# Mixture of experts on one core: Strassen's form for all first layers from the start, and the gates spread over the partitions by transfers

## The chip, the cores and the metric

The kernel runs on one core of a Trainium2 chip. The metric is the device time of one execution in microseconds (us); lower is better. The kernel before takes 3385.79 us, the median of three runs (3379.62 to 3386.1). A core has a matrix engine (TensorE, PE in the profile; PEld is its weight load), VectorE (DVE), ScalarE (ACT) and GpSimd (POOL), and SyncE (SP), which here only issues transfers. Each engine works through its own instructions in order; between engines, semaphores hold an instruction back until its operands are there.

## What is computed

Two layers, in fp32, over eight images of 256 channels and 32 x 32 positions. Layer 0 is group norm and a pooled convolution and attention hybrid; the change leaves it alone. Layer 1 takes the positions as 1024 tokens of 256 numbers: layer norm, attention with one head, residual; then layer norm and a mixture of eight experts, residual. The experts are where the change is (x has the shape 8 images x 1024 tokens x 256; batch norms are folded into a scale and a bias per channel in the kernel):

```python
feat = jnp.mean(x, axis=0)
w = jax.nn.softmax(feat @ Wr + br, axis=-1)
h = jnp.einsum('bfd,edh->bfeh', x, W1) + b1
h = jax.nn.relu(_bn(h, g1, be1, m1, v1))
h = jnp.einsum('bfeh,ehk->bfek', h, W2) + b2
h = jax.nn.relu(_bn(h, g2, be2, m2, v2))
y = jnp.einsum('bfeh,ehd->bfed', h, Wo) + bo
return jnp.einsum('bfed,fe->bfd', y, w)
```

The gates `w` (1024 tokens x 8 experts) come from the mean over all eight images. So they are known only when the last image's attention and layer norm are done, while first and second layers of the experts can run before.

## The kernel before, in words

**The work of the experts.** Activations lie with channels on the 128 partitions, in two halves `k`. The function `experts` (line 1988) cuts the eight images into 16 tiles `hn` of half an image ([128, 2, 512]), and each tile meets eight experts: 128 units, unit `i` being expert `i % 8` of tile `i // 8`. A unit has three layers:

- `first(i)` (2126) is the plain first layer: two `half`s (2107), each of two fp32 matmul calls of 128 x 128 by 512 columns into one PSUM bank "bank" (four buffers, each call is a pair of matmul records in the trace), and a relu on ScalarE that empties it into `h1`.
- `second(i, staged)` (2133) has the same form with `w2` into `h2`. With `staged`, `h2` is stored to its place `h2d[i]` in DRAM; `fetch(i)` (2144) brings it back.
- `weigh(i)` (2236) multiplies `h2` by the gates of its expert, a tile `gb` of [128, 8 experts, 1024 tokens] with each gate repeated on all partitions, and makes the combinations `t3`; `third(i)` (2242) adds the product with `wo` into the PSUM banks "y", over all eight experts of a tile. After the eighth the residual is added on VectorE and the tile is stored to `out`.

**Strassen's form.** `first7(i)` (2222) and `third` use seven products of quarter size for a 256 x 256 matrix by 512 columns, in place of eight (Winograd's form of Strassen's scheme): `products` (2188) issues seven matmul calls of 256 columns into four banks, `weights` (2171) makes four sums of a weight's blocks on GpSimd once per expert (`s1e`, `s3e`), `combined` (2180) makes four combinations of the operand on VectorE (`t1` once per tile, `t3` once per unit), and `sums` (2209) puts the products together: a copy `p1c` on ScalarE and four sums on VectorE that read the banks (`c`, `u`). In `first7` ScalarE's relu then reads `c`. So a plain first layer's banks are freed by ScalarE, and those of a Strassen first layer by VectorE.

**The order of the work.** The order on each engine is fixed when the program is built, by a planner, the class `Flow` (655). It models every engine's time with `cost` (710) and puts instructions on each engine in the order in which they are called. Threads are generators that yield what they need next; `step(pace)` runs those that are runnable, up to a credit of modelled TensorE time (8.0 per step, `PACE2`), and `finish` drives them until a condition holds. When `experts` starts, layer 1's attention and norms of the last images still run as threads. `experts` adds the thread `gates` (2036): it sums the eight images on VectorE (`featsum`, the other images come through one buffer `feat`), multiplies by the router's weights, forms the softmax and transposes it to `gt`, [8 experts, 1024 tokens]. Then, for each of 16 pairs of half and expert, a matmul with the selecting matrix `sel` spreads one row of `gt` over 128 partitions, and ScalarE copies it from PSUM to `gb`. Last, four products with `bo` give `added`.

While the gates are not complete, the loop at line 2153 runs first and second layers of units 0, 1, 2 and so on, with a planner's step after each; all are plain, and their `h2` go to DRAM. It comes to 22 first and 21 second layers. Then `early.close()` gives back the memory of attention (l1) and of the gates' working tiles (wg), the pool `wp3` and the banks "y" take its place, `s3e` and `s1e` are made, units 0 and 1 are fetched, and the last loop (2277) begins: a third layer, a second layer and a Strassen first layer per turn, and a further third layer while units are still staged in DRAM. 106 first layers have Strassen's form.

The transfers of SP leave in program order: SP waits at each for what it needs, so one that waits holds those behind it.

Of the kernel before, what the change touches and what calls it, by code (L numbers as in the profile page):

```python
# [13 lines left out]
PSUM = bass.MemoryType.PSUM  # L14
# [1970 lines left out]
        advance(after(nb - 1), 10**6)  # L1985


def experts(tc, kit, nb, t2, hn, h2d, w1c, w2_d, wo_d, bnvec, bo_d, gate_d, wrc, consts8, out, f, outer, ended, early):

# [10 lines left out]
    with ExitStack() as ctx:  # L2000
# [22 lines left out]
        f.sp.dma_start(wr, wrc.rearrange("p k e -> p (k e)"))  # L2023
        br = T(wg, [P, NE], "br")
        f.sp.dma_start(br, gate_d[:, 2 * NE :])
        sel = T(wg, [NE, NE * P], "sel")
        f.sp.dma_start(sel, consts8[:, : NE * P])
        bo = T(wg, [NE, C], "bo")
        f.sp.dma_start(bo, bo_d)
        for e in range(NE):  # L2030
            f.sp.dma_start(wo[e], wo_d[:, e])
        gt = T(wg, [NE, HW], "gt")
        gb = T(wp, [P, NE, HW], "gates")
        gated = []

        def gates():

            featsum = T(wp, [P, 2, HW], "featsum")  # L2040
            for b in range(nb):
                yield None, lambda: ended[0] > b, None
                if b == 0:
                    f.sp.dma_start(featsum, hn[0])
                else:
                    h = T(wg, [P, 2, HW], "feat")
                    f.sp.dma_start(h, hn[b])
                    for k in range(2):
# [13 lines left out]
            gate = T(wg, [P, 8, NE], "gate")  # L2062
            yield "DVE", (ps,), None
            f.ve.tensor_scalar(gate, ps, 1.0 / nb, None, ALU.mult)
            f.ve.tensor_tensor(gate, gate, br[:, None, :].to_broadcast([P, 8, NE]), ALU.add)
            red = T(wg, [P, 8], "red")
            f.ve.tensor_reduce(red, gate, AX.X, ALU.max)
            f.ve.tensor_tensor(gate, gate, red.unsqueeze(2).to_broadcast([P, 8, NE]), ALU.subtract)
            yield "ACT", (gate,), None
            f.act.activation(gate, gate, AF.Exp)  # L2070
            yield "DVE", (gate,), None
            f.ve.tensor_reduce(red, gate, AX.X, ALU.add)
            f.ve.reciprocal(red, red)
            f.ve.tensor_tensor(gate, gate, red.unsqueeze(2).to_broadcast([P, 8, NE]), ALU.mult)
            for half in range(2):
                yield "PE", (gate,), "sm"
                ps = T(shared, [P, 512], "sm", bufs=2)
                for ft in range(4):
                    f.pe.transpose(ps[:NE, ft * P : (ft + 1) * P], gate[:, 4 * half + ft, :], kit.ident)
                yield "DVE", (ps,), None  # L2080
                f.ve.tensor_copy(gt[:, half * 512 : half * 512 + 512], ps[:NE, :])
            for half in range(2):
                sl = slice(half * 512, half * 512 + 512)
                for e in range(NE):
                    yield "PE", (gt,), "sm"
                    ps = T(shared, [P, 512], "sm", bufs=2)
                    f.pe.matmul(ps, lhsT=sel[:, e * P : (e + 1) * P], rhs=gt[:, sl], start=True, stop=True)
                    f.act.activation(gb[:, e, sl], ps, AF.Copy)
            added = T(wp, [P, 2, HW], "featsum")
            for m in range(2):  # L2090
                for half in range(2):
                    sl = slice(half * 512, half * 512 + 512)
                    yield "PE", (gt,), "sm"
                    ps = T(shared, [P, 512], "sm", bufs=2)
                    f.pe.matmul(ps, lhsT=bo[:, m * P : (m + 1) * P], rhs=gt[:, sl], start=True, stop=True)
                    f.act.activation(added[:, m, sl], ps, AF.Copy)
            gated.append(added)
# [32 lines left out]
                half(h, w1[e], e, xs[tile_i], 0, 1, m)  # L2130
            loaded(i)

        def second(i, staged):
            _, e, _, _ = where(i)
            h, src = T(work, [P, 2, 512], "h2", bufs=5), h1s.pop(i)
            for m in range(2):
                half(h, w2[e], e, src, 2, 3, m)
                yield
            if staged:
                f.sp.dma_start(h2d[i], h)  # L2140
            else:
                h2s[i] = h

        def fetch(i):
            if i not in h2s:
                h = h2s[i] = T(work, [P, 2, 512], "h2", bufs=5)
                f.sp.dma_start(h, h2d[i])

        total = 2 * nb * NE
        f.spawn(gates(), 7)  # L2150
        n1 = n2 = n3 = 0

        while not gated and n2 < NSTAGED:
            first(n1)
            n1 += 1
            f.step((PACE2, PACE2))
            if n1 > 1:
                for _ in second(n2, True):
                    pass
                n2 += 1  # L2160
                f.step((PACE2, PACE2))
        f.finish(lambda: gated)
        early.close()
        wp3 = ctx.enter_context(tc.tile_pool(name="w3", bufs=1, side="right"))
        psum_y = ctx.enter_context(tc.tile_pool(name="psum_y", bufs=1, space=PSUM, side="right"))

        def blocks(w):

            return w[:, 0, :P], w[:, 1, :P], w[:, 1, P:]

        def weights(w, tag):
            s = T(wp3, [P, 4, P], tag)
            a11, a12, a22 = blocks(w)
            f.pool.tensor_tensor(s[:, 0, :], w[:, 0, P:], a22, ALU.add)
            f.pool.tensor_tensor(s[:, 1, :], s[:, 0, :], a11, ALU.subtract)
            f.pool.tensor_tensor(s[:, 2, :], a11, w[:, 0, P:], ALU.subtract)
            f.pool.tensor_tensor(s[:, 3, :], a12, s[:, 1, :], ALU.subtract)
            return s

        def combined(h, tag):  # L2180

            t = T(wp3, [P, 4, C], tag, bufs=2)
            f.ve.tensor_tensor(t[:, 0:2, :], h[:, :, C:], h[:, 0, :].rearrange("p (n q) -> p n q", n=2), ALU.subtract)
            f.ve.tensor_tensor(t[:, 2, :], h[:, 1, C:], t[:, 0, :], ALU.subtract)
            f.ve.tensor_tensor(t[:, 3, :], h[:, 1, :C], t[:, 2, :], ALU.subtract)
            return t
# [21 lines left out]

        def sums(banks):

            c = T(wp3, [P, 4, C], "c", bufs=2)
            u = T(wp3, [P, 2, C], "u", bufs=2)
            p26, p57, p34 = (banks[i].rearrange("p (u q) -> p u q", u=2) for i in (0, 2, 3))
            p1 = T(wp3, [P, 1, C], "p1c", bufs=2)
            f.act.activation(p1[:, 0, :], banks[1][:, :C], AF.Copy)
            f.ve.tensor_tensor(c[:, 0::2, :], p1.to_broadcast([P, 2, C]), p26, ALU.add)
            f.ve.tensor_tensor(u, c[:, 2:3, :].to_broadcast([P, 2, C]), p57, ALU.add)
            f.ve.tensor_tensor(c[:, 3, :], u[:, 1, :], p57[:, 0, :], ALU.add)
            f.ve.tensor_tensor(c[:, 1:3, :], u, p34, ALU.add)
            return c.rearrange("p (m n) q -> p m (n q)", m=2)  # L2220

        def first7(i):
# [10 lines left out]
            if e == NE - 2 and tile_i + 1 in xs:  # L2233
                ts[tile_i + 1] = combined(xs[tile_i + 1], "t1")

        def weigh(i):
            _, e, _, sl = where(i)
            h = h2s[i]
            f.ve.tensor_tensor(h, h, gb[:, e : e + 1, sl].to_broadcast([P, 2, 512]), ALU.mult)
            h2s[i] = h, combined(h, "t3")  # L2240

        def third(i):
            tile_i, e, b, sl = where(i)
# [10 lines left out]
                f.sp.dma_start(out[b].rearrange("(k p) n -> p k n", p=P)[:, :, sl], t)  # L2254
                ys.pop(tile_i)

        s1, s3 = {}, {}
        for i in range(NE):
            s3[i] = weights(wo[i], f"s3e{i}")
            e = (n1 + i) % NE  # L2260
            s1[e] = weights(w1[e], f"s1e{e}")

        def thirds(count):
            nonlocal n3
# [7 lines left out]
                    n3 += 1  # L2272

        for i in range(2):
            fetch(i)
        weigh(0)
        while n3 < total:
# [18 lines left out]
def tile_conv_attn_hybrid(  # L2296
# [34 lines left out]
    t1, t2, hn = ([T(dram, [P, 2, HW], f"{name}_{b}") for b in range(nb)] for name in ("t1", "t2", "hn"))  # L2331
    w1c = T(dram, [P, NE, 2, C], "w1c")
    wrc = T(dram, [P, 2, NE], "wrc")
    h2d = [T(dram, [P, 2, 512], f"h2_{i}") for i in range(2 * nb * NE)]

    assert 8 * nb <= NBOUND
    bnvec = T(cpool, [P, 4 * 2 * NE], "bnvec")
    bounds = [T(cpool, [P, NBOUND], f"bound{i}") for i in range(2)]
    flag = T(cpool, [P, 1], "flag")
    last = partial(experts, tc, kit, nb, t2, hn, h2d, w1c, w2_d, wo_d, bnvec, bo_d, gate_d, wrc, consts8, out)  # L2340
    with ExitStack() as early:
        l1 = early.enter_context(tc.tile_pool(name="l1", bufs=1, side="right"))
        shared = early.enter_context(tc.tile_pool(name="psum_l1", bufs=1, space=PSUM, side="right"))
# [130 lines left out]
```

## Time and profile before

The profiled execution has a span of 3379.9 us and a mean TensorE clock of 0.980 of full speed. Instructions are named by the tiles they write and read, since all of them are recorded by one helper line (L668): "bank<-hn,w1e" is a plain first layer or a Strassen one's product of the operand itself, "bank<-t,s1e" a product of two sums, "y<-..." the third layers, "sm" the banks of attention and of the gates.

| Engine | busy us | share of the span | instructions |
|---|---|---|---|
| TensorE | 3195.0 | 95% | 15270 |
| VectorE | 2267.8 | 67% | 3890 |
| ScalarE | 1695.4 | 50% | 2222 |
| GpSimd | 520.7 | 15% | 644 |

| Group (out<-in) | count | mean ns |
|---|---|---|
| TensorE bank<-h,w2e, 512 columns | 1024 | 594 |
| TensorE bank<-hn,w1e, 256 and 512 columns | 600 | 447 |
| TensorE bank<-t,s1e, 256 columns | 636 | 379 |
| ScalarE h<-bank, relu of 512 columns | 300 | 772 |
| VectorE c<-p1c,bank, 512 columns | 106 | 688 |
| VectorE h<-h,gates, 1024 columns | 128 | 1227 |
| transfers h<-h, 512 KB | 76 | 4100 from issue to landing |
| transfers hn<-hn, 512 KB | 16 | 5500 from issue to landing |

Busy times are sums over the whole span, and only a part of the span is the change's. The experts begin near 1990 us, attention's last work and the gates run until 2272 us, and the rest, to 3380 us, is the loop of thirds, seconds and firsts.

### The profile page before, as it was taken

To read this page: it belongs to the slowest core of one execution; us is meant where nothing else is said; L and a number is where in the kernel's file an instruction comes from. 1 tells how busy PE (TensorE), PEld (TensorE's weight loads), DVE (VectorE), ACT (ScalarE), POOL (GpSimd) and SP (SyncE) were. 2 spreads that over 40 slices of the span, in tenths; PEclk is the share of its full clock that TensorE was granted. 3 is DMA by queue.
4 is the path that set the end of the run, shared out by engine and by line. 5 is a ranking of instruction groups with operands and counts; after the bars stand their busy time and mean duration, and the time that the engine had idled before them with its cause. 6 is when DMAs were issued, how large, how long until landed. Compare 5 with 4: busy or idle time off the path is not lost.

```text
span 3379.9 us, 39921 instructions
## 1 busy us (share of the span) xinstructions
PE 3195.0 (95%) x15270; PEld 1780.3 (53%) x15270; DVE 2267.8 (67%) x3890; ACT 1695.4 (50%) x2222; POOL 520.7 (15%) x644
## 2 busy tenths in 40 slices
PE   8687899899899999899899989999999999999997
PEld 4322245344345345344344446637777777777775
DVE  6687787886886887877875444207766666666665
ACT  4476676676576666666665533342223333333332
POOL 2211414213213214213212100013000000000000
PEclk9798999999999999999999999999999999999999
DMA  2366646647656566556557573214430100000000
GB/s 73 82 127 158 137 93 155 139 97 154 128 128 127 124 150 126 114 130 126 113 122 154 113 207 132 78 67 139 162 106 19 35 22 19 19 19 19 19 13 20
DMA packets 102328, 335.37 MB, mean 99 GB/s; under 512 B 12576, under 2 KB 37928, under 8 KB 78896
## 3 DMA queue, kind: packets, MB, share of 16 engines
q0 software_dynamic: 28608, 179.85, 27.7%
q1 hardware_dynamic: 70160, 150.91, 13.1%
q8 instruction: 122, 2.00, 0.2%
q10 hardware_dynamic: 3360, 1.97, 0.2%
q14 instruction: 78, 0.64, 0.1%
HBM read 97.28 MB, written 70.26 MB: 50 GB/s over the span
## 4 chain that ended last, share of the span: by engine, by line
PE 66%; ACT 2%; issue 2%; DMA 1%; DVE 1%; POOL 1%; SPq 0%; POOLq 0%; ACTq 0%; DVEq 0%
PE bank L668 25%; PE sm L668 14%; PE y L668 11%; PE sc L668 6%; PE sx L668 6%; PE pv L668 5%; ACT pt L668 2%; DMA pt<-pt 1%; POOL rstd L668 0%; DVE t L668 0%; DMA h<-h 0%; DMA hn<-hn 0%; POOL pt L668 0%; DVE rec L668 0%; DMA t<-pt 0%
## 5 line engine op out<-in xcount | busy, mean ns | idle before, releaser
L668 ACT ACTIVATE pt<-sc 128x2048 f32<-128x2048 f32 (+1 forms) x384 | 720.2, 1876 | 324.0 <-PE sc L668 275.2
L668 DVE SCALAR_TENSOR_TENSOR acc<-p,vec,acc 128x225 f32<-128x225 f32 (+7 forms) x928 | 527.0, 575 | 28.3 <-ACT acc L668 3.8
L668 PE MATMUL sc<-q,kn 32*128 32x512 f32 (+1 forms) x3072 | 444.8, 649 | 94.2 <-ACT pt L668 92.9
L668 DVE TENSOR_TENSOR pt<-pt,pt 128x1024 f32<-128x1024 f32 x320 | 387.6, 1255 | 139.8 <-DMA pt<-pt 122.1
L668 PE MATMUL bank<-h,w2e 128*128 128x512 f32 x1024 | 479.9, 594 | 0.0
L668 ACT ACTIVATE h<-bank,bnvec 128x512 f32<-128x512 f32 x300 | 231.5, 772 | 479.0 <-PE bank L668 458.1
L668 PE MATMUL pv<-pt,vt 128*32 128x512 f32 (+1 forms) x3072 | 420.5, 620 | 0.0
L668 ACT ACTIVATE h<-c,bnvec 128x512 f32<-128x512 f32 x212 | 161.1, 807 | 320.6 <-DVE c L668 320.6
L668 POOL DMA_DIRECT2D pt<-pt x192 | 174.3, 909 | 779.3 <-ACT pt L668 619.8
L668 DVE TENSOR_TENSOR c<-p1c,bank 128x512 f32<-128x512 f32 x106 | 72.9, 688 | 309.1 <-PE bank L668 309.0
L668 PEld LDWEIGHTS bank<-h,w2e 128*128 128x128 f32 x1024 | 194.4, 191 | 151.9 <-issue 140.0
L668 PEld LDWEIGHTS sc<-q,kn 32*128 32x128 f32 (+1 forms) x3072 | 116.0, 178 | 285.2 <-ACT pt L668 184.4
L668 PEld LDWEIGHTS pv<-pt,vt 128*32 128x32 f32 (+1 forms) x3072 | 60.8, 108 | 300.9 <-issue 289.5
L668 POOL TENSOR_TENSOR rstd<-rstd,mhalf 128x4 f32<-128x4 f32 (+2 forms) x88 | 105.8, 1203 | 689.1 <-DVE rstd L668 592.6
L668 DVE TENSOR_TENSOR h<-h,gates 128x1024 f32<-128x1024 f32 x128 | 157.1, 1227 | 71.4 <-DMA h<-h 64.3
L668 PE MATMUL bank<-hn,w1e 128*128 128x256 f32 (+1 forms) x600 | 191.2, 447 | 11.0 <-DMA hn<-hn 11.0
L668 PE MATMUL y<-t,s3e 128*128 128x256 f32 x768 | 187.5, 380 | 0.0
L668 PE MATMUL sm<-y,t 128*128 128x256 f32 x752 | 180.4, 385 | 0.0
L668 PEld LDWEIGHTS bank<-hn,w1e 128*128 128x128 f32 x600 | 114.3, 192 | 101.1 <-issue 93.7
L668 PEld LDWEIGHTS sm<-y,t 128*128 128x128 f32 x752 | 137.9, 190 | 56.1 <-issue 34.4
L668 ACT ACTIVATE p<-sm 128x512 f32<-128x512 f32 (+1 forms) x151 | 88.5, 586 | 144.8 <-PE sm L668 121.5
L668 PE MATMUL bank<-t,s1e 128*128 128x256 f32 x636 | 154.7, 379 | 2.8 <-DVE t L668 2.8
(306 smaller groups left out, 4672.5 us busy)
## 6 DMA issues: line engine op xcount, KB each, us to landing
pt<-pt POOLq DMA_DIRECT2D x160, 1024.0 KB, 7.4
h<-h SPq DMA_DIRECT2D x76, 512.0 KB, 4.1
xi<-in_x_dram SPq DMA_DIRECT2D x16, 512.0 KB, 6.3
t<-t SPq DMA_DIRECT2D x8, 1024.0 KB, 9.3
res<-t SPq DMA_DIRECT2D x32, 256.0 KB, 4.2
t<-res SPq DMA_DIRECT2D x32, 256.0 KB, 5.3
hn<-res SPq DMA_DIRECT2D x32, 256.0 KB, 2.9
hn<-hn SPq DMA_DIRECT2D x16, 512.0 KB, 5.5
```

The source lines that it names most:

```text
L668: ins = fn(*args, **kwargs)
```

## The change

It has two parts.

1. Strassen's form from the beginning. The sums `s1e` of all experts are made when `experts` starts, and the buffers of `combined` and `sums` lie in the pools that exist from the start. Only the first three first layers stay plain; all others are `first7`. One planner's step comes ahead of the first of them. A function `ahead` does one first and one second layer, and is called once more ahead of each of the two fetches with which the last loop begins, so that 25 first and 24 second layers are issued ahead of the third layers.
2. The gates by transfers. The 16 selecting matmuls, their 16 copies on ScalarE and the load of `sel` go. `gt` is stored to DRAM (`gtd`); `gb` is allocated in `wp3`, after the memory of attention has been given back, and filled by 16 transfers of SP, each of which reads one row's half (2 KB) for all 128 partitions and writes 256 KB. `f.split` lets the planner see the 16 parts as separate tiles. That `gb` lies in `wp3` is what makes room in `wp` for the first part's tiles. The first transfer waits for the store of `gt` and for the last reader of the memory that `gb` takes over.

The diff, without what only moves:

```diff
-        sel = T(wg, [NE, NE * P], "sel")
-        f.sp.dma_start(sel, consts8[:, : NE * P])
...
-        gb = T(wp, [P, NE, HW], "gates")
...
-            for half in range(2):
-                sl = slice(half * 512, half * 512 + 512)
-                for e in range(NE):
-                    yield "PE", (gt,), "sm"
-                    ps = T(shared, [P, 512], "sm", bufs=2)
-                    f.pe.matmul(ps, lhsT=sel[:, e * P : (e + 1) * P], rhs=gt[:, sl], start=True, stop=True)
-                    f.act.activation(gb[:, e, sl], ps, AF.Copy)
+            f.sp.dma_start(gtd, gt)
             added = T(wp, [P, 2, HW], "featsum")
...
-        while not gated and n2 < NSTAGED:
-            first(n1)
-            n1 += 1
-            f.step((PACE2, PACE2))
-            if n1 > 1:
-                for _ in second(n2, True):
-                    pass
-                n2 += 1
-                f.step((PACE2, PACE2))
...
-            c = T(wp3, [P, 4, C], "c", bufs=2)
-            u = T(wp3, [P, 2, C], "u", bufs=2)
+            c = T(work, [P, 4, C], "c", bufs=2)
+            u = T(work, [P, 2, C], "u", bufs=2)
...
-            p1 = T(wp3, [P, 1, C], "p1c", bufs=2)
+            p1 = T(work, [P, 1, C], "p1c", bufs=2)
...
+        s1 = {e: weights(w1[e], f"s1e{e}", wp) for e in range(NE)}
+
+        def ahead():
+            nonlocal n1, n2
+
+            (first if n1 < 3 else first7)(n1)
+            if n1 == 0:
+                ts[0] = combined(xs[0], "t1")
+            n1 += 1
+            f.step((PACE2, PACE2))
+            if n1 > 1:
+                for _ in second(n2, True):
+                    pass
+                n2 += 1
+                f.step((PACE2, PACE2))
+
+        f.step((PACE2, PACE2))
+        while not gated and n2 < NSTAGED:
+            ahead()
+        f.finish(lambda: gated)
+        early.close()
+        wp3 = ctx.enter_context(tc.tile_pool(name="w3", bufs=1, side="right"))
+
+        gb = T(wp3, [P, NE, HW], "gates")
+        f.split(gb, *(512 * i for i in range(1, 2 * NE)))
+        for part in range(2):
+            sl = slice(part * 512, part * 512 + 512)
+            for e in range(NE):
+                f.sp.dma_start(gb[:, e, sl], gtd[e : e + 1, sl].to_broadcast([P, 512]))
+        psum_y = ctx.enter_context(tc.tile_pool(name="psum_y", bufs=1, space=PSUM, side="right"))
...
-            h2s[i] = h, combined(h, "t3")
+            h2s[i] = h, combined(h, "t3", wp3)
...
-        s1, s3 = {}, {}
+        s3 = {}
         for i in range(NE):
-            s3[i] = weights(wo[i], f"s3e{i}")
-            e = (n1 + i) % NE
-            s1[e] = weights(w1[e], f"s1e{e}")
+            s3[i] = weights(wo[i], f"s3e{i}", wp3)
...
         for i in range(2):
+            ahead()
             fetch(i)
         weigh(0)
```

More of the change, by code (lines that the diff above doesn't have):

```diff
@@ L1985, in layer1_general, with experts @@
         advance(after(nb - 1), 10**6)
-def experts(tc, kit, nb, t2, hn, h2d, w1c, w2_d, wo_d, bnvec, bo_d, gate_d, wrc, consts8, out, f, outer, ended, early):
+def experts(tc, kit, nb, t2, hn, h2d, w1c, w2_d, wo_d, bnvec, bo_d, gate_d, wrc, consts8, gtd, out, f, outer, ended, early):
     with ExitStack() as ctx:
@@ L2131, in first, with weights @@
             loaded(i)
[L2133 to L2151, printed above, removed]
-        while not gated and n2 < NSTAGED:
-            first(n1)
-            n1 += 1
-            f.step((PACE2, PACE2))
-            if n1 > 1:
-                for _ in second(n2, True):
-                    pass
-                n2 += 1
-                f.step((PACE2, PACE2))
[L2162 to L2165, printed above, removed]
         def blocks(w):
             return w[:, 0, :P], w[:, 1, :P], w[:, 1, P:]
-        def weights(w, tag):
-            s = T(wp3, [P, 4, P], tag)
+        def weights(w, tag, pool):
+            s = T(pool, [P, 4, P], tag)
             a11, a12, a22 = blocks(w)
@@ L2178, in weights, with combined @@
             return s
-        def combined(h, tag):
-            t = T(wp3, [P, 4, C], tag, bufs=2)
+        def combined(h, tag, pool=work):
+            t = T(pool, [P, 4, C], tag, bufs=2)
             f.ve.tensor_tensor(t[:, 0:2, :], h[:, :, C:], h[:, 0, :].rearrange("p (n q) -> p n q", n=2), ALU.subtract)
@@ L2234, in first7, with second, fetch @@
                 ts[tile_i + 1] = combined(xs[tile_i + 1], "t1")
+        def second(i, staged):
+            _, e, _, _ = where(i)
+            h, src = T(work, [P, 2, 512], "h2", bufs=5), h1s.pop(i)
+            for m in range(2):
+                half(h, w2[e], e, src, 2, 3, m)
+                yield
+            if staged:
+                f.sp.dma_start(h2d[i], h)
+            else:
+                h2s[i] = h
+        def fetch(i):
+            if i not in h2s:
+                h = h2s[i] = T(work, [P, 2, 512], "h2", bufs=5)
+                f.sp.dma_start(h, h2d[i])
+        total = 2 * nb * NE
+        f.spawn(gates(), 7)
+        n1 = n2 = n3 = 0
+        s1 = {e: weights(w1[e], f"s1e{e}", wp) for e in range(NE)}
[24 more added lines that the diff above has]
+        psum_y = ctx.enter_context(tc.tile_pool(name="psum_y", bufs=1, space=PSUM, side="right"))
         def weigh(i):
@@ L2333, in tile_conv_attn_hybrid @@
     wrc = T(dram, [P, 2, NE], "wrc")
+    gtd = T(dram, [NE, HW], "gtd")
     h2d = [T(dram, [P, 2, 512], f"h2_{i}") for i in range(2 * nb * NE)]
@@ L2339, in tile_conv_attn_hybrid @@
     flag = T(cpool, [P, 1], "flag")
-    last = partial(experts, tc, kit, nb, t2, hn, h2d, w1c, w2_d, wo_d, bnvec, bo_d, gate_d, wrc, consts8, out)
+    last = partial(experts, tc, kit, nb, t2, hn, h2d, w1c, w2_d, wo_d, bnvec, bo_d, gate_d, wrc, consts8, gtd, out)
     with ExitStack() as early:
```

## The prediction, made before the changed kernel ran

> **What bounds the kernel now.** I read the page's busy shares and chain first: is one engine the limit, and in which matmuls.
>
> ```profile
> PE 3195.0 (95%) x15270; PEld 1780.3 (53%) x15270; DVE 2267.8 (67%) x3890; ACT 1695.4 (50%) x2222; POOL 520.7 (15%) x644
> ...
> PE 66%; ACT 2%; issue 2%; DMA 1%; DVE 1%; POOL 1%; SPq 0%; POOLq 0%; ACTq 0%; DVEq 0%
> PE bank L668 25%; PE sm L668 14%; PE y L668 11%; PE sc L668 6%; PE sx L668 6%; PE pv L668 5%; ACT pt L668 2%; DMA pt<-pt 1%; POOL rstd L668 0%; DVE t L668 0%; DMA h<-h 0%; DMA hn<-hn 0%; POOL pt L668 0%; DVE rec L668 0%; DMA t<-pt 0%
> ```
>
> TensorE leads, and "bank" (the experts' first and second layers) is the largest part. The average says nothing of the stage that the diff touches, so next the busy times by stretch (PE, PEld, DVE, ACT, POOL, clock, DMA share, GB/s):
>
> ```profile
> core 0: us, PE busy (x) PEld busy (x) DVE busy (x) ACT busy (x) POOL busy (x), PEclk, DMA share, GB/s
> ...
> 2150.00:2200.00 50.00, 50.00 (x158) 28.98 (x157) 14.08 (x29) 16.90 (x26) 3.01 (x4) 1.00 0.25 89
> ...
> 2222.00:2272.00 50.00, 50.00 (x109) 18.91 (x108) 0.00 (x0) 24.89 (x37) 0.28 (x1) 1.00 0.12 48
> 2272.00:2285.00 13.00, 5.33 (x13) 2.92 (x12) 3.23 (x5) 1.77 (x3) 12.45 (x26) 0.79 0.62 219
> 2285.00:2300.00 15.00, 12.17 (x49) 9.47 (x49) 14.18 (x20) 2.33 (x4) 14.61 (x22) 0.95 0.15 55
> ```
>
> From 1998 to 2272 TensorE is never idle, while VectorE works a third of the time or less. So matmul time that goes from this stretch goes from the kernel. There is one hole, at 2272 to 2285, where the third layers begin. After it TensorE is full again (210.00 of 210 us, then 830.00 of 830). Then TensorE's timeline for single costs (start, us, operation):
>
> ```profile
> 1997.70 6.37 PE L668 MATMUL bank<-hn,w1e 128*128 128x512 f32 x8 [10.98 <-DMA hn<-hn]
> ...
> 2189.47 3.60 PE L668 MATMUL bank<-h,w2e 128*128 128x512 f32 x8
> 2192.91 3.60 PE L668 MATMUL bank<-hn,w1e 128*128 128x512 f32 x8
> ...
> 2225.29 1.98 PE L668 MATMUL sm<-gt,sel 8*128 8x512 f32 x4
> 2227.20 3.70 PE L668 MATMUL bank<-h,w2e 128*128 128x512 f32 x8
> 2230.83 1.98 PE L668 MATMUL sm<-gt,sel 8*128 8x512 f32 x4
> ...
> 2282.89 2.04 PE L668 MATMUL y<-h,wo 128*128 128x256 f32 x4 [7.67 <-DVE h L668]
> 2284.72 2.32 PE L668 MATMUL y<-t,s3e 128*128 128x256 f32 x6
> ...
> 2294.62 1.56 PE L668 MATMUL bank<-t,s1e 128*128 128x256 f32 x6 [2.83 <-DVE t L668]
> ```
>
> Start to start, a plain layer costs 3.44 us (2189.47 to 2192.91), and one with a pair of selecting matmuls beside it 5.54 (2225.29 to 2230.83).
>
> [...] of the w1e loads, 256 KB each, the first lands in 3.5 us, the median, with others ahead of it, in 6.6. [...] after the 7.67 us hole four matmuls take 1.83 us start to start (2282.89 to 2284.72), and 0.86 when warm. [...]
>
> **The change, part by part.**
>
> *Strassen's form earlier.* Before, 22 first layers are plain: the matmuls bank<-hn,w1e of 128x512 are 176, 8 each. After, by the built order, 3 are. So 19 change form. Plain: 3.43 us in the chain of waits (8 matmuls). Strassen's: 14 matmuls of 256 columns; in the steady loop a Strassen first, a second and a third layer take 9.477 us together (2514.25 to 2523.73 in the chain), first and third have the same 14, so (9.477 - 3.43)/2 = 3.02. Saved 0.42 x 19 = 8.0 us, all of it on a full TensorE.
>
> *Selecting matmuls.* 16 go, in 8 pairs: 8 x (5.54 - 3.44) = 16.8 us of a full TensorE. Their 16 evictions (597 ns) leave ScalarE, which waited anyway: nothing. The two pairs with bo stay.
>
> *Start.* In the after order four Q-K matmuls (sm<-y,t, 1.73 us start to start) stand ahead of the first layer that waits 10.98 us for hn. They need nothing of that load, so they fall into its idle time: 1.7 us. The 32 s1e sums now run on GpSimd here: 32 x about 0.5 us = 16 us from w1e's landing near 1998, to 2014. GpSimd's next row, the rstd, ran at 2013.88 before, so it moves by a microsecond or two, and the first of its results is wanted by TensorE at about 2025: nothing.
>
> *VectorE's new part.* Each Strassen first layer adds four sums (688 + 688 + 420 + 680 ns = 2.5 us): 47 us more in a stretch of 277 us where VectorE had some 75. It has the room. But the release of the matmul banks moves from ScalarE to VectorE, and what waits in VectorE's queue now holds TensorE. Queued there: the feature sums (7 pairs of 1.22 us, each behind a 1 MB load with a single buffer) and six reciprocals of 1.76 us. In the built order the first sum of each first layer must end before the second half of the following second layer, some 3.4 us after its operands are there: that covers a reciprocal or a pair of sums, not a late load. The first pair stands ahead of the first reciprocal, whose result gates TensorE near 2025.1 (1997.7 plus 27.4 us of matmuls). Its load landed at 2024.0 and comes about 2 us earlier now, with less ahead of it in the queue: 2022 + 2.44 + 1.76 + 0.6 = 2026.8, a wait of 1.7. I take 3 us for the whole stretch; ends: 0, and all thirteen in full, 7 x 2.44 + 6 x 1.76 = 27.6.
>
> *The hole.* Before, from 2274.95 it costs 7.9 us idle (the fetch of h2 is issued only after the last store), 2.8 for the t1 sums, and 1.8 of halved clock: 12.6. After, t1 is there, and two more units (2 x (3.02 + 3.43) = 12.9 us) stand ahead of the third layers. But SP's order is: store 21, sixteen gate fills of 256 KB, a load of hn, store 22, and only then the first fetch, each waiting for the transfer eight places earlier. No fill of this kind is in the trace. The nearest is the weights' loads, the same size and number:
>
> ```profile
> 1991.46 0.32 SPq L668 DMA_DIRECT2D w1e<-w1c  x1
> ...
> 2002.37 0.33 SPq L668 DMA_DIRECT2D w2e<-in_w_dram  x1
> 2004.40 0.52 SPq L668 DMA_DIRECT2D hn<-hn  x1
> ```
>
> Sixteen and one hn in 11.2 us, the next at 12.9. Count from the end of second layer 21: its eviction ends at 1.0, fills from 1.4, hn at 14.3, fetch at 15; landing 5.5 (hn<-hn's median), so 20.2. The gates' product (1.22 us) lets the third layer begin at 21.5; TensorE is free at 12.9. Idle 8.6, clock 1.8: 10.4, against 12.6: saved 2.2. The s3e sums on GpSimd (32 x 0.46 us = 15) are done by then: nothing. What I don't know is whether 128 reads of one DRAM row run like 128 reads of different rows. Lower end: everything up to the fetch is 6.3 MB, at the some 390 GB/s that the weights' loads hold (DMA view, 2000 to 2006) 16.1 us, so one or two us less. Upper end: the rivals.
>
> *Afterwards* the catch-up has three more staged tiles, full on TensorE with or without them (12.50 us per turn, 3.02 more than 9.477, just the third layer added): nothing.
>
> Sum: 8.0 + 16.8 + 1.7 - 3 + 2.2 = 25.7; 3385.8 - 25.7 = **3360**.
>
> **Rivals.**
>
> *VectorE holds TensorE.* All thirteen blocks fall through: 27.6 instead of 3, 3385, no change. For: strict order, single feature buffer. Against: the planner places each instruction by its estimate of when its operands are there, and VectorE stays under half busy.
>
> *Fills at half speed.* [...] the 12.9 us of fills become some 25, the hole 12 longer: 3372. For: all engines read one 2 KB row. Against: eight fills are under way, from rows 4 KB apart.
>
> *Fills one after another.* If each lasts its 3.5 us alone, 16 take 56, 43 more: 3403, slower than before. The fetch behind them waits with them, and nothing else can feed TensorE, since the third layers come next in its order.
>
> **How the numbers follow.** My forecast 0.63, half-speed fills 0.12, VectorE 0.11, serial fills 0.14. Low 3350: no VectorE wait (3 less) and a hole of about 4 us in place of 10.4. High 3383: it takes in half-speed fills and most of VectorE's case, and leaves out the serial fills. Faster (below 3379): 0.63 + 0.12 and a little of VectorE's case, 0.77; the rest of that case same, 0.09; slower 0.14.
>
> **What would show it.** Full TensorE from 1998 to the hole, with that stretch and the hole ending so that the steady loop runs 9.477 us per turn: right. Waits of matmuls "bank" on VectorE's c or u: the size of the 3 us. The gates' fills: landing near 6.6 us each is my case, 12 or more the half-speed case. The idle before y<-h,wo: 8.6 predicted. If that wait is long, the prediction fails there; if the mixed stretch has idle time in many places, in VectorE's term.

## The result and the profile after

The changed kernel takes 3363.76 us, the median of four runs (3361.5 to 3366.81), against 3385.94 before: a ratio of 0.9938, with an interval of 0.9921 to 0.9955. Repeated beside the first experiments it was 0.9939 (0.9925 to 0.9952). So it is faster by some 21 us. 3360 was forecast, 25.7 us less than before; both the direction and the size hold, and the sum was 4 or 5 us too good.

The page of the changed kernel, its busy shares and its chain, to be read against those of before:

```profile
PE 3175.6 (94%) x15352; PEld 1801.8 (54%) x15352; DVE 2311.2 (69%) x3972; ACT 1688.4 (50%) x2225; POOL 511.1 (15%) x644
...
PE 64%; DMA 2%; ACT 2%; issue 2%; DVE 1%; POOL 1%; SPq 0%; ACTq 0%; POOLq 0%; DVEq 0%
```

TensorE is busy for 19.4 us less, although it has 82 matmuls more (19 layers more in Strassen's form, 125 instead of 106, are 6 more each; 32 selecting ones are gone); transfers have gone from 1% to 2% of the chain. Where that is, the busy times by stretch tell (columns as before: length, PE, PEld, DVE, ACT, POOL, clock, DMA share, GB/s):

```profile
2028.00:2040.00 12.00, 8.29 (x31) 6.62 (x31) 9.32 (x12) 0.89 (x3) 0.00 (x0) 0.86 0.61 184
2040.00:2230.00 190.00, 189.81 (x752) 139.37 (x751) 95.45 (x180) 72.88 (x126) 13.65 (x15) 1.00 0.29 102
2230.00:2248.00 18.00, 18.00 (x69) 11.94 (x68) 8.24 (x17) 5.79 (x9) 0.00 (x0) 0.81 0.14 56
2248.00:2279.00 31.00, 31.00 (x105) 18.24 (x103) 12.21 (x21) 15.42 (x24) 13.93 (x32) 1.00 0.45 134
2279.00:2290.00 11.00, 0.03 (x1) 0.03 (x1) 1.28 (x2) 0.78 (x1) 0.00 (x0) 0.61 1.04 404
...
2300.00:2510.00 210.00, 210.00 (x840) 159.32 (x839) 153.46 (x234) 57.58 (x88) 0.00 (x0) 1.00 0.42 146
```

The stretch with Strassen's form (2040 to 2230) is full but for 0.2 us, with VectorE half busy: the new sums hold TensorE up nowhere in it but for that. From 2300 on TensorE is full again. What is left is one hole, 2279 to 2290, and in it the transfer engines are saturated (share 1.04, 404 GB/s). TensorE's timeline names the waits:

```profile
2002.02 8.54 PE L668 MATMUL bank<-hn,w1e 128*128 128x512 f32 x16 [8.55 <-DMA hn<-hn]
...
2031.91 0.88 PE L668 MATMUL sm<-diag,con 128*128 128x256 f32 x2 [3.71 <-ACT sm L668]
...
2228.08 1.03 PE L668 MATMUL bank<-hn,w1e 128*128 128x256 f32 x4
...
2231.10 3.60 PE L668 MATMUL bank<-h,w2e 128*128 128x512 f32 x8
2234.53 1.03 PE L668 MATMUL bank<-hn,w1e 128*128 128x256 f32 x4
...
2237.55 4.20 PE L668 MATMUL sm<-wr,featsum 128*128 128x8 f32 x32
2241.60 6.49 PE L668 MATMUL bank<-h,w2e 128*128 128x512 f32 x8
...
2275.40 3.60 PE L668 MATMUL bank<-h,w2e 128*128 128x512 f32 x8
2289.97 2.08 PE L668 MATMUL y<-h,wo 128*128 128x256 f32 x4 [10.97 <-DVE h L668]
2291.84 2.77 PE L668 MATMUL y<-t,s3e 128*128 128x256 f32 x6
```

The three lines from 2228.08 on give the price of a layer from start to start: 3.02 us in Strassen's form, 3.43 us for the plain second layer behind it. SP's timeline shows what was on the queue ahead of the last wait:

```profile
2253.24 0.29 SPq L668 DMA_DIRECT2D gtd<-gt  x1
2256.26 10.99 SPq L668 DMA_DIRECT2D h<-h  x2
2267.42 11.79 SPq L668 DMA_DIRECT2D gates<-gtd  x16
2279.56 0.57 SPq L668 DMA_DIRECT2D hn<-hn  x1
2280.27 3.27 SPq L668 DMA_DIRECT2D h<-h  x5
```

The fills start behind the store of unit 21 and take 11.8 us to issue; the fetch that the first third layer needs leaves as the second of the last row, at 2281.14. In the trace it lands at 2288.51, and VectorE's gates' product begins at 2288.69; the first of the fills, the only one that this product needs, had landed at 2272.12. So the product waits for the fetch. The prediction has each transfer of SP wait for the one eight places earlier: the fetch left 0.02 us after the fill eight places ahead of it had landed (2281.12).

**A ledger.** Executions differ by several us in the layer ahead of the experts, which the change does not touch. So I count from the last matmul group sm<-att,mt ahead of the experts (1983.12 before, 1988.15 after) to the end: 1396.8 and 1376.9 us, 19.9 less. The sums of that stretch close. Matmuls removed: 8.0 + 16.8 = 24.8 by the prediction's prices. TensorE's idle times: 10.98 + 7.67 + 2.83 = 21.5 before, 8.55 + 3.71 + 0.19 + 10.97 = 23.4 after: 1.9 more. Time above what the same groups take at a granted clock of 1.00, from start to start, in the groups that follow an idle time or the small router products (sm<-wr,featsum): 6.4 before, 9.4 after: 3.0 more. 24.8 - 1.9 - 3.0 = 19.9.

### The profile page after: what moved, and what is told of

Its sections match the earlier page's. It is cut to its first block, busy times and chain, and to the rows that moved or that the text cites. A ratio compares the mean times of both kernels' runs of the same rounds, so it can differ in the third digit from the quotient of the medians.

```text
span 3365.0 us, 40262 instructions
## 1 busy us (share of the span) xinstructions
PE 3175.6 (94%) x15352; PEld 1801.8 (54%) x15352; DVE 2311.2 (69%) x3972; ACT 1688.4 (50%) x2225; POOL 511.1 (15%) x644
## 3 DMA queue, kind: packets, MB, share of 16 engines
q1 hardware_dynamic: 74192, 161.40, 13.9%
q10 hardware_dynamic: 3360, 1.97, 0.2%
## 4 chain that ended last, share of the span: by engine, by line
PE 64%; DMA 2%; ACT 2%; issue 2%; DVE 1%; POOL 1%; SPq 0%; ACTq 0%; POOLq 0%; DVEq 0%
PE bank L668 23%; PE sm L668 13%; PE y L668 12%; PE sc L668 6%; PE sx L668 6%; PE pv L668 5%; ACT pt L668 2%; DMA pt<-pt 1%; DMA hn<-hn 0%; DMA feat<-hn 0%; POOL rstd L668 0%; DVE rec L668 0%; DMA gates<-gtd 0%; DMA w1e<-w1c 0%; POOL pt L668 0%
## 5 line engine op out<-in xcount | busy, mean ns | idle before, releaser
L668 ACT ACTIVATE h<-bank,bnvec 128x512 f32<-128x512 f32 x262 | 201.3, 769 | 385.7 <-PE bank L668 374.0
L668 ACT ACTIVATE h<-c,bnvec 128x512 f32<-128x512 f32 x250 | 189.9, 807 | 385.7 <-DVE c L668 385.7
L668 DVE TENSOR_TENSOR c<-p1c,bank 128x512 f32<-128x512 f32 x125 | 85.9, 687 | 350.9 <-PE bank L668 349.9
L668 PE MATMUL bank<-t,s1e 128*128 128x256 f32 x750 | 183.2, 380 | 0.2 <-ACT h L668 0.2
L668 PEld LDWEIGHTS y<-t,s3e 128*128 128x128 f32 x768 | 146.8, 191 | 20.2
L668 PEld LDWEIGHTS bank<-t,s1e 128*128 128x128 f32 x750 | 143.1, 191 | 20.2 <-ACT h L668 0.6
```

What stands on the lines that cost most here:

```text
L668: ins = fn(*args, **kwargs)
```

## The experiments

"Rest" below is the time from that last matmul group to the end in the run's own trace; medians and ratios are of the timed runs, five rounds each.

**The changed kernel again.** No edit.

> The changed kernel once more, beside the others on one chip. Theory of the trace: counted from the last matmul before the experts, the change takes 24.8 us of matmuls away and gives back 4.9 us in idle time and lower clock, so about 20 us: 3366 us, and a ratio of 0.994. If the difference of the medians (22 us) is nearer the truth: 3363.

Measured: 3363.56 us, ratio 0.9939 (0.9925 to 0.9952); its trace has a rest of 1370.1 us, 26.7 less than before's. So one trace is not enough for the small terms: here TensorE waits 0.0 us at the first diag matmul instead of 3.71, and the router's products with the second layer behind them run at a clock of 1.00, against 0.67 in the first trace. The hole is the same: 11.02 us. The same account closes for this trace too: 24.8, and 0.6 less idle time and 1.3 less slow clock than before, are 26.7.

```profile
2026.44 0.67 PE L668 MATMUL sm<-diag,con 128*128 128x256 f32 x2
...
2279.98 2.07 PE L668 MATMUL y<-h,wo 128*128 128x256 f32 x4 [11.02 <-DVE h L668]
```

**The fetches ahead of the fills.** Is the hole SP's order, or the fills?

```diff
         f.finish(lambda: gated)
+        for i in range(2):
+            fetch(i)
         early.close()
...
         for i in range(2):
             ahead()
-            fetch(i)
```

> The fetches of units 0 and 1 are issued ahead of the sixteen fills of the gates' tile; all else is as in the changed kernel. Theory Q (the hole is SP's queue: the third layer waits for a fetch that lies behind the fills, not for the gates): the fetches land during the last second layers, TensorE goes from the second layer 23 straight to the first third layer, and the hole with its slow clock goes: 11.0 us idle and 2.6 us of clock less, about 3351 us. Theory G (the first third layer has to wait for the fills themselves, because they are slow or come late): the hole stays near 11 us and the time near 3364. Theory S (the share of the transfer engines is what counts, in whatever order): some 3 us of hole less, 3360.

Measured: 3359.51 us, ratio 0.9929 (0.9916 to 0.9942), rest 1366.1. The first two third layers now follow the last second layer without a gap, at 2264.29, while the last fill was issued only at 2266.1. So theory G falls, and the forecast of theory Q (3351) was missed as well: a hole of 6.33 us comes back two units later. By its time alone this run would fit theory S (3360); the run with four loads ahead, below, decides against that. SP's and VectorE's timelines show what the new hole is:

```profile
2268.08 1.67 SPq L668 DMA_DIRECT2D h<-h  x3
2270.06 0.81 SPq L668 DMA_DIRECT2D t<-t  x1
...
2266.96 0.88 DVE L668 TENSOR_TENSOR t<-h,t 128x256 f32<-128x256 f32 x2
2279.15 1.23 DVE L668 TENSOR_TENSOR t<-t,featsum 128x1024 f32<-128x1024 f32 x1 [11.31 <-DMA t<-t]
2280.29 1.22 DVE L668 TENSOR_TENSOR h<-h,gates 128x1024 f32<-128x1024 f32 x1
```

The third layer of unit 0 also loads the first residual (t2). That load still stood behind the fills, and took 9.1 us to land. Its sum stands in VectorE's order ahead of the gates' product for unit 2, which needs nothing of it, and TensorE waits for that product. It is not the whole of the hole: the fetch of unit 2, the third of the row h<-h above, was left behind the fills too. The store ahead of it landed at 2275.86 and the residual behind it at 2279.13, so without the residual's sum in the way some 2 to 5 of the 6.33 us would have stayed (an estimate from these landings).

**Half of the fills ahead.** The eight fills of the second half of the tokens are moved behind the fetches:

```diff
-        for part in range(2):
+        def fill(part):
...
+        fill(0)
...
             ahead()
             fetch(i)
+        fill(1)
         weigh(0)
```

> Only the eight fills for the first half of the tokens stand ahead of the fetches; the other eight follow them. Theory Q: the fetch is issued 8 x 0.74 = 5.9 us earlier and finds less ahead of it, so the hole falls from 11.0 to about 5, and the time to about 3357. Theory G: as in the changed kernel, 3364, since the first fill lands at the same time in both. Theory S: the hole stays within 2 us of 11.

Measured: 3357.28 us, ratio 0.9927 (0.9914 to 0.994), rest 1369.8; the hole is 5.98 us in place of 10.97, then 1.20 and 0.22 behind the fills that were moved. Eight fills less ahead are 5.0 us less hole, near the 6 that theory Q gives. With the 1.42 us that come back the idle time falls by 3.6 us; the median falls by 6.3, more than the holes explain, and the rest by 7.1 against the first trace of the changed kernel and by 0.3 against the repeat.

**All four loads ahead of the fills.** The fetches of units 0 to 2 and the first residual:

```diff
         f.finish(lambda: gated)
+        for i in range(3):
+            fetch(i)
+        residual = {0: T(work, [P, 2, 512], "t2")}
+        f.sp.dma_start(residual[0], t2[0][:, :, :512])
         early.close()
...
-                t = T(work, [P, 2, 512], "t2")
-                f.sp.dma_start(t, t2[b][:, :, sl])
+                t = residual.pop(tile_i, None)
+                if t is None:
+                    t = T(work, [P, 2, 512], "t2")
+                    f.sp.dma_start(t, t2[b][:, :, sl])
```

> As the run with the fetches first, and in addition the fetch of unit 2 and the load of the first residual (t2) stand ahead of the fills. Theory Q, as that run's trace has amended it (the hole is whatever VectorE's strict order meets first behind the fills: there it was the residual's load, 9.1 us, whose sum stands ahead of the gates' product for unit 2): nothing that the first three third layers need lies behind the fills, TensorE has no idle time from 2200 us into the loop, and 11.0 + 2.6 us go from the changed kernel: about 3350 us, some 5 us more than the fetches alone gave. Rival (the fills themselves hold up the gates' products): a hole of 5 us or more stays, now with the gates' transfers named.

Measured: 3346.85 us, ratio 0.9882 (0.9868 to 0.9896), rest 1360.2. The hole is gone. The stretches of its trace around the place where it was:

```profile
2257.00:2273.00 16.00, 16.00 (x52) 9.72 (x52) 6.05 (x11) 8.53 (x15) 13.89 (x32) 1.00 0.64 227
2273.00:2290.00 17.00, 16.90 (x68) 12.42 (x67) 12.94 (x19) 4.01 (x6) 0.00 (x0) 1.00 0.95 344
2290.00:2300.00 10.00, 10.00 (x43) 7.87 (x43) 8.88 (x16) 3.35 (x5) 0.00 (x0) 1.00 0.44 159
```

The transfer engines are nearly as loaded as before (0.95), with the same sixteen fills; they only come in another order. So theory S falls too. The new order moves 16.7 us by the medians, and 16.6 and 9.8 by the rests of the two traces of the changed kernel; the hole and the slow clock behind it were 13.6. What the medians have beyond that is not traced to a place. Since the fetch of unit 2 and the residual were moved together, the run does not tell their shares apart.

**No units beside the fills.** What the two calls of `ahead` hide:

```diff
         for i in range(2):
-            ahead()
             fetch(i)
```

> The two units of first and second layers ahead of the fetches are left out there (they come later, in the loop): the fetches stand directly behind the fills. Theory Q: the fetch is issued about 1.7 us earlier than in the changed kernel (no load of hn and no store ahead of it) and lands a little faster, but TensorE's 12.9 us of work no longer lie beside the fills: the hole is about 20 us, and the time 9 us longer: 3373. Theory G' (the hole has a fixed length, whatever lies ahead of the third layers): 3364.

Measured: 3370.83 us, ratio 0.9955 (0.9942 to 0.9968), rest 1383.5; 7.3 us more than the changed kernel where 9 were forecast. The hole is 21.5 us, and here the profile names the fetch as what VectorE's product waited for:

```profile
2281.04 1.23 DVE L668 TENSOR_TENSOR h<-h,gates 128x1024 f32<-128x1024 f32 x1 [23.23 <-DMA h<-h]
2282.41 2.05 PE L668 MATMUL y<-h,wo 128*128 128x256 f32 x4 [21.50 <-DVE h L668]
```

The hole is 10.5 us longer for 12.9 us of work taken from beside the fills; the difference is that the fetch left 1.1 us sooner after the end of the second layer 21 (14.1 us, not 15.2) and the product began 6.2 us after its issue, not 7.5. So the work beside the fills shortens the hole nearly one for one. A hole of fixed length is ruled out.

**The gates by transfers alone.** All first layers ahead of the last loop stay plain:

```diff
-            (first if n1 < 3 else first7)(n1)
+            first(n1)
```

> The gates' part of the change alone: all first layers ahead of the last loop are plain (22 of them, 3 in the changed kernel), the gates still come by transfers. Theory: 19 x 0.42 = 8.0 us of matmuls come back on a full TensorE, and the hole gets about 0.8 us shorter since the two units behind the fills last longer; the banks are freed by ScalarE again. 3364 + 7 = 3371 us, counted from the last matmul before the experts to the end 7 us more than the changed kernel. Rival (VectorE's new sums hold TensorE at many places): no slower than the changed kernel, 3364 or less.

Measured: 3365.61 us, ratio 0.9941 (0.9928 to 0.9954), rest 1376.3: no slower than the changed kernel that can be told, where 7 us were expected. Not because VectorE held TensorE in the other: the hole is 6.60 us here, 4.4 shorter. The planner placed the units differently against the gates' products. TensorE leaves the last bo product at 2251.36, with no second layer between it and the two units of `ahead`, and the fills start at 2251.51, at once. In the changed kernel it leaves the last bo product at 2262.39, a second layer (unit 21) follows, and the fills wait behind its store until 2267.42. So this run compares two orders, and does not measure Strassen's part.

**Strassen's part with no hole in the way.** The same edit in the run with the four loads ahead.

```diff
-            (first if n1 < 3 else first7)(n1)
+            first(n1)
```

> All four loads ahead of the fills as before, so that there is no hole in either, and all first layers ahead of the last loop plain: Strassen's part alone, without the hole that differed in the run with plain layers. Theory: 19 x 0.42 = 8.0 us more than with Strassen's form from the beginning: 3346.9 + 8.0 = 3355 us. Rival (VectorE's new sums hold TensorE elsewhere and eat the gain): 3347 to 3350.

Measured: 3353.74 us, ratio 0.9916 (0.9901 to 0.9931), rest 1366.9: 6.9 us more than with Strassen's form by the medians, 6.6 by the rests, where 8.0 were forecast for the 19 layers. The times alone don't fix this better than to several us: by the ratios, each to the kernel before on its own chip, it is 11.5 us, with an interval from about 4 to 19. So the rival's 3347 to 3350 is unlikely. The price per layer is better read from the trace of the changed kernel, 3.02 us against 3.43. One small idle time is in this run and not in the other: 1.49 us for the sums `t1`.

**The selecting matmuls in two blocks.** `sel` and `gt` move to the pool that stays; the fills are replaced by eight matmuls with eight copies ahead of each unit:

```diff
+        def spread(part):
+            sl = slice(part * 512, part * 512 + 512)
+            for e in range(NE):
+                ps = bank()
+                f.pe.matmul(ps, lhsT=sel[:, e * P : (e + 1) * P], rhs=gt[:, sl], start=True, stop=True)
+                f.act.activation(gb[:, e, sl], ps, AF.Copy)
...
         for i in range(2):
+            spread(i)
             ahead()
             fetch(i)
```

> The gates' tile lies where the changed kernel has it, but is filled by the 16 selecting matmuls and ScalarE's 16 copies, eight ahead of each of the two units before the third layers; no fills. Strassen's form stays from the beginning. Theory: 16 matmul calls put 16.8 us (8 x 2.1) on TensorE, or somewhat less in two blocks of eight; but nothing stands ahead of the fetches on SP, so the hole of 13.6 us goes: 3364 + 16.8 - 13.6 = 3367 us. Rival (the hole is not the fills' work): the hole stays, 3380.

Measured: 3378.93 us, ratio 0.9981 (0.9971 to 0.999). The expectation missed by 12 us. Two things were not foreseen. The fetch of unit 1 stands behind the store of unit 23 and lands late, which leaves a hole of 4.86 us. And the blocks cost more than their matmuls: from start to start 9.6 and 11.3 us for what was priced at 16.8 together. The stretches of this trace are the first block, the unit behind it, the second block, and the unit behind that one:

```profile
2253.30:2263.00 9.70, 9.70 (x18) 3.64 (x17) 0.00 (x0) 4.96 (x8) 9.31 (x23) 0.73 0.34 110
2263.00:2272.00 9.00, 9.00 (x22) 5.79 (x22) 2.47 (x4) 3.17 (x5) 1.32 (x4) 0.72 0.00 0
2272.00:2283.30 11.30, 11.30 (x17) 4.14 (x16) 0.00 (x0) 4.96 (x8) 0.00 (x0) 0.62 0.25 93
2283.30:2292.00 8.70, 8.70 (x23) 5.93 (x23) 4.56 (x7) 3.03 (x5) 0.00 (x0) 0.70 0.00 1
```

TensorE is busy throughout, and the granted clock is 0.73 and 0.62 in the blocks, 0.72 and 0.70 in the units behind them. The first four matmuls behind either block take 1.87 us from start to start, against 0.86 in the stretches at a clock of 1.00. The trace gives the form of the selecting matmuls as 8*128: 8 rows.

**The selecting matmuls in pairs.** The same with the four loads ahead, the matmuls in pairs between layers and half layers, into the banks of the third layers:

```diff
+        def spread():
+            for n in range(2 * NE):
+                part, e = divmod(n, NE)
...
+                ps = T(psum_y, [P, 512], f"y{n % 4}")
...
+                if n % 2:
+                    yield
...
-            ahead()
+            ahead(lambda: next(pairs, None))
```

> The gates by 16 selecting matmuls and 16 copies once more, now in pairs between the layers and half layers (into the banks of the third layers) and with the four loads ahead, so that no transfer is in the way: the selecting matmuls' price alone. Theory (in blocks of eight they ran 9.6 and 11.3 us and the granted clock fell to 0.62 to 0.73; between full matmuls they do not): 8 x 2.1 = 16.8 us more than the run with the four loads ahead, 3346.9 + 16.8 = 3364 us, at a clock near 1.0 in that stretch. Rival (the price of the blocks is theirs wherever they stand): 26 us more, 3373.

Measured: 3363.33 us, ratio 0.9946 (0.993 to 0.9962): 16.5 us more than with the fills, where 16.8 were forecast. By the rests it is 15.1 (1375.3), by the ratios 21.7 with an interval from about 14 to 29. There is no hole. The clock in the pairs' stretch is 0.94, and what was lost of it lies behind the one place where two pairs stand together (the six matmuls bank<-t,s1e take 2.51 us from start to start there, and 1.30 behind the first pair, at 2259.16):

```profile
2269.06 3.70 PE L668 MATMUL y<-gt,sel 8*128 8x512 f32 x8
2272.68 1.13 PE L668 MATMUL bank<-hn,w1e 128*128 128x256 f32 x4
2273.65 2.72 PE L668 MATMUL bank<-t,s1e 128*128 128x256 f32 x6
```

So the price of the selecting matmuls holds with no transfer in the way; the rival's 26 us is not excluded by the ratios, but the trace shows no slow clock in this stretch other than there.

**The loads of wo later.** The eight loads of `wo` go behind the feature sum's first two loads:

```diff
-        for e in range(NE):
-            f.sp.dma_start(wo[e], wo_d[:, e])
...
         f.step((PACE2, PACE2))
+        ahead()
+        for e in range(NE):
+            f.sp.dma_start(wo[e], wo_d[:, e])
         while not gated and n2 < NSTAGED:
```

> The eight loads of wo (2 MB) are issued behind the first two images' loads for the feature sum, not ahead of them. Theory V (VectorE's queue: the reciprocal that TensorE waits for at the start stands behind a feature sum whose load comes late): the load lands about 5 us earlier, TensorE's 3.7 us of idle time at the first diag matmul and the slow clock after it (1.8 us) go: 5.5 us less, about 3358 us. Rival (the wait is ScalarE's or the softmax's own chain): the idle time stays at 3.7 us and the time near 3364.

Measured: 3358.91 us, ratio 0.993 (0.9917 to 0.9943), rest 1372.9. By its time it can't be told apart from the changed kernel. Its trace is clear on the step: the first feature sum starts 31.4 us after the last matmul group ahead of the experts, against 39.0 and 37.5 in the two traces of the changed kernel, and then the reciprocal waits for its operand (TensorE's product and ScalarE's step on it, which the line names), no longer TensorE for the reciprocal:

```profile
2006.83 2.36 DVE L668 TENSOR_TENSOR featsum<-featsum,feat 128x1024 f32<-128x1024 f32 x2 [14.10 <-DMA feat<-hn]
2011.48 1.76 DVE L668 RECIPROCAL rec<-sm 128x256 f32<-128x256 f32 x1 [2.30 <-ACT sm L668]
```

**The two together.** All four loads ahead of the fills, and the loads of wo later, by the edits shown:

```diff
+        ahead()
+        for e in range(NE):
+            f.sp.dma_start(wo[e], wo_d[:, e])
...
+        for i in range(3):
+            fetch(i)
+        residual = {0: T(work, [P, 2, 512], "t2")}
+        f.sp.dma_start(residual[0], t2[0][:, :, :512])
```

> The run with all four loads ahead of the fills, and the loads of wo behind the feature sum's first two loads. Theory: the two are independent; the wait at the first diag matmul (0 to 3.7 us in the executions so far, 1.3 on average) goes too: 3346.9 - 1.3 = 3345.5 us, the fastest of all. Rival: the later wo loads push the feature sum's third image back and cost it elsewhere: 3347 or more.

Measured: 3345.88 us, ratio 0.9888 (0.9873 to 0.9904), rest 1355.2. There is no wait at the diag matmul and no hole. (In the ten other traces with the loads of `wo` at their old place, the changed kernel's two among them, that wait is 0.0 to 3.71 us, 1.4 on average.) The intervals of this run and of the four loads alone overlap, so that the second edit's gain of a microsecond stays unproven as a time. Either kernel beats both the one before and the changed one, by some 39 and 17 us.

## Why the prediction was right, and where it was off

- **Matmuls, 24.8 forecast.** Right within what can be told. With the hole out of the way, Strassen's form brought 6.9 of the 8.0 and the selecting matmuls cost 16.5 of 16.8: 23.4 by the medians, 21.7 by the rests. The 8.0 itself was rounded up: 3.43 - 3.02 is 0.41, and 19 of these are 7.8.
- **Start, 1.7 forecast.** Right. The idle time ahead of the first layer fell from 10.98 to 8.55 us with four Q-K matmuls of 1.73 in it, and in the repeat to 9.48; the first layer starts 13.9 and 14.8 us after the last matmul group, against 14.6, so the moved work is free. The first layer's slow clock, 2.8 us before, 1.5 and 2.8 after, was not in the term; with it the start gained 3.7 us in the first trace and 1.5 in the repeat.
- **VectorE's queue, 3 forecast.** Right in its mechanism. The wait came where it was named: TensorE at the diag matmul, for a reciprocal behind a feature sum whose load was late. It was forecast at 1.7 us and measured at 3.71 and 0.0. In the first trace the diag matmul could start 43.8 us after the last matmul group ahead of the experts, as forecast (43.7); TensorE got there at 40.1, where 42.0 was forecast. With 1.8 us of slow clock behind it, the first trace has 5.7 for the term, and the repeat 0.35. In these sums are two short waits for a bank, 0.19 and 0.35, in which the profile names ScalarE; in the first trace ScalarE itself had waited 5.66 us for a sum `c` that stood behind feature sums in VectorE's order. That the stretch left VectorE two thirds of its time was true on average (26% busy from 1998 to 2272), but in its first 52 us, where this wait lies, it was busy for 42%. Of the thirteen blocks that the rival wanted in full, one fell through. The rival of 3385 is ruled out by the stretch from 2040 to 2230.
- **The hole, a gain of 2.2 forecast, a loss of 1.2 measured.** Here the sum failed. The order was right to a fraction of a microsecond: the fetch was put 15 us after the end of the second layer 21 (2265.93), and left at 2281.14, 15.2 after it. Two sizes were off. The fetch's landing was taken at 5.5 us, the median of the loads hn<-hn; the gates' product that waits for it began at 2288.69, 7.5 us after the issue, with the transfer engines saturated at 404 GB/s by what had been issued ahead. And the slow clock behind the hole cost 2.6 us, not 1.8. In these runs it does not follow the length of the idle time: behind 21.5 us (the run with no units beside the fills) it cost 1.5, behind 4.86 us (the selecting matmuls in two blocks) 2.6. Idle time and clock together are 13.6 us in place of 10.4. The fetch is 512 KB, and each fill ahead of it 256 KB.
- **The fills themselves.** The price of a row read for 128 partitions was open: the trace of the kernel before has no such fill, and the rival's half speed was an assumption. In the changed kernel's trace the summary of the transfers that write the gates reads, in us:

```profile
DMA to landing us min/median/max: 4.7/6.4/7.7
```

  6.6 was the median of the w1e loads of the same size, 12 or more, by the author's estimate, the sign of half speed. Both rivals on the fills, half speed (3372) and one after another (3403), fall: the median landing, 6.4 us, is near the 6.6 of the w1e loads, and the sixteen are issued within 11.8 us.
- **Not in the prediction at all:** the clock around the router's products, which cost 1.8 us before, 3.5 in the first trace after and 0.1 in the repeat. It differs from execution to execution of the same kernel, so that a difference of this size between two traces is no sign of the change.

That 26.7 us in the repeat lies so near the 25.7 of the forecast is in part luck: the wait at the diag matmul and the router's slow clock were absent in that execution, which outweighs what the hole gave less than forecast. So the gain was the removed matmuls, and of the hole only the place in time changed: two units more of work were put beside it, and sixteen fills were put ahead of the fetch that ends it.

## What to carry to other kernels

When one engine issues many transfers together with loads that another is about to need, issue those loads first: here, with the same sixteen fills behind four loads, the kernel took 17 us less by the medians, 13.6 of which are the hole and its slow clock. After such a move, follow the next wait in each engine's order; here a hole of 6.33 us came back two units later, through VectorE's order and two loads that had been left behind the fills. And where a planner sets the order, two edits are not additive: test a part in a kernel whose other waits are gone.

## What the runs showed of the hardware that was not expected

In the run with the selecting matmuls in two blocks, eight calls in a row of the form 8*128, TensorE was busy without a gap, and the granted clock was 0.73 and 0.62 in the blocks; the first four matmuls of 256 columns of the Strassen layers behind took 1.87 us from start to start, against 0.86 at a clock of 1.00. In pairs between full layers the same matmuls ran at a clock of 1.00 in the kernel before (2220 to 2272) and 0.94 in the run with pairs (2256 to 2287). Whether the lower clock comes of their 8 rows or of their number in a row was not shown. The 32 router's products of 8 columns, with the second layer behind them, ran at 0.67 in the first trace of the changed kernel, and at 1.00 in the repeat and in the run with both edits.

Idle times of TensorE in the experts' part differ in what follows them. Behind 1.19 us (four loads ahead), 1.24 (half of the fills ahead), 2.33 (two blocks) and 2.83 (the kernel before), the matmuls lost 0.2 us or less; behind 3.16 (no units beside the fills), 3.71 (the changed kernel, first trace) and all longer ones of these traces, up to 21.5, they lost between 1.5 and 3.1 us. No trace has one between 2.83 and 3.16 there, and what the granted clock follows was not shown.
